# Summing attention values for twelve heads at a time instead of eight, with a third set of weight buffers, in one stage of a two-layer network

## The chip, the cores and the metric

The kernel runs on one core of a Trainium2 chip. The metric is device time in microseconds (us), the median of three runs. TensorE appears as PE in the profile (its weight loads as PEld), VectorE as DVE, ScalarE as ACT, GpSimd as POOL, SyncE, which issues most DMAs, as SP.

## The reference

Two layers on x of shape (16, 512, 128), each adding an attention-like block and an expert block to x:

```python
x = x + _L0_attn_ref(xn, ...) + _L0_ffn_ref(xn, ...)   # xn: layernorm of x
xn = _layernorm(x, axis=-1)
x = x + _L1_attn_ref(xn, ...) + _L1_ffn_ref(xn, ...)
```

The layer-0 attention is a memory that is trained by gradient steps over eight chunks. The layer-0 expert block is a convolution, a full attention of 16 heads of width 8, and eight dense experts of width 512. The change lies in the layer-1 attention, which runs a causal attention twice with the same keys and values:

```python
def _causal_attn(q, k, v):
    scores = jnp.einsum('bthd,bshd->bhts', q, k) * scale
    scores = jnp.where(mask, scores, -jnp.inf)
    attn = jax.nn.softmax(scores, axis=-1)
    return jnp.einsum('bhts,bshd->bthd', attn, v)
ctx = _causal_attn(q, k, v)
q2 = conv1d(ctx)                 # width 3, along the sequence
ctx2 = _causal_attn(q2, k, v)
out = ctx2.reshape(b, s, d) @ out_w.T + out_b
```

The layer-1 expert block routes each token to 8 of 32 experts.

## The kernel before, in words

**Turns.** The whole program is written out ahead of time by Python generators. `Turns.run` (line 284) steps every live generator once per turn, in the order of its priority; PE's order is exactly the order in which matmuls are written. Priority 0 is `tops` (`largest`, line 379): score matmuls (`s<-qx,kx`, rows 64*128) whose row maxima DVE takes (lines 396, 403, 404). Priority 1 is `back` (`weighted`, line 428): score matmuls again, transposed (`s<-kx,qx`), exponentials on ACT into a buffer `e` (line 476), the causal cut on POOL (line 484), and the value matmuls `pc<-e,vp`, which use the array as four strips of 32 columns (128*32). Later priorities hold the rest: `summed` (line 498), projections, the middle stage between the layers, and the layer-0 experts (`ffn`, line 547), whose matmuls are `phe` and `pye`. At a turn's end `fill` (line 199) adds a matmul without use if PE had little to do.

**A unit of attention.** A batch has four units in layer 1 (two passes, two halves of the heads), each of eleven turns, since a causal unit is walked in eleven steps (`widths`, line 360): four steps of width 512, four of 384, two of two times 256, one of four times 128. A step gives 2, 2, 4 or 8 heads, 32 in all. New units begin every eleven turns and a batch every 44, so the stage repeats itself every eleven turns. After the maxima of a unit, lines 410 and 411 make `mp` on DVE, PE transposes it (`tpm`, line 418), and it goes by DMA to DRAM (`top`) and back into `qx`. The unit's `back` starts some turns later and needs it.

**Values.** `weighted` keeps finished heads in the list `old`. In each step, after its scores, `tail` (line 453) looks whether at least `pools["heads"]` heads are waiting and, if so, writes value matmuls for them in groups of four, at most two groups. What is left after the eleventh step is written by `summed`. The `e` buffers come in turn from the pools in `pools["weights"]`, three from each. In layer 1 there are two pools: `att` and `mid`, later `att` and `fb`. `fb` lies where layer 0's buffers `fa` lay; it is opened when layer 0's last batch has been handed over (line 1531), but used only after the last middle stage. `lent` holds the heads whose buffer is in `mid`; the last stage begins when none is left.

**Experts.** `ffn` writes units (`first`: two matmul records of 512 columns and a ReLU on ACT; `second`: eight records of 128) as a running credit allows. Line 633 makes it write them in pairs, and none in a turn that had values, unless more than three are due.

**PSUM.** Seven banks with the tag `bank` (line 178) go round for scores and all other results; an eighth holds `pc`.

Of the kernel before, what the change touches and what calls it, by code (L numbers as in the profile page):

```python
# [73 lines left out]
def bc(ap, axis, n):  # L74

    u = ap.unsqueeze(axis)
    shape = list(u.shape)
    shape[axis] = n
    return u.to_broadcast(shape)
# [3 lines left out]
def network(ctx: ExitStack, tc: tile.TileContext, a, out):  # L83
# [56 lines left out]
    pools, done, locks, clock, newest, cleared, held, read, cell = {}, {}, set(), [0], [None], [None], [0], [0], []  # L140
# [11 lines left out]
    def acquire(name):  # L152
        while name in locks:
            yield
        locks.add(name)
# [21 lines left out]
    def work(name):  # L177
        return pools["ps"].tile([P, 512], F32, tag="bank", bufs=7, name=name)
# [10 lines left out]
    def mm(o, lhsT, rhs, start=True, stop=True):  # L189
        n = int(np.prod(rhs.shape[1:]))  # L190
        if lhsT.dtype == FR:
            load_ns[0] += 0.5 * (0.45 * n + 105)
        else:
            t = 0.42 * n if lhsT.shape[-1] == 32 and n >= P else 2 * max(0.834 * n, 110)
            load_ns[0] += t
            array_ns[0] += t
        nc.tensor.matmul(o, lhsT=lhsT, rhs=rhs, start=start, stop=stop)  # L197
# [71 lines left out]
    def ends(stage, name):  # L269
        yield from stage  # L270
        mark(*name)
# [88 lines left out]
    def widths(causal):  # L360

        for i in range(TB):
            n = S if not causal else S - i * P
            per = {S: 1, 3 * P: 1, 2 * P: 2, P: 4}[n]
            for t in range(0, NH, per):
                yield i, n, per, t
# [61 lines left out]
    def weighted(slot, vp, c, causal, cn, name):  # L428


        q, k, _ = slot
        yield from acquire("p2")
        cnv = cn.rearrange("p t (a c j d) -> p (t a) c j d", c=2, j=2, d=DH)
        old, last = [], []
        got = []

        def values(heads):
            for head in heads:
                kt, n, t, r, e = head
                lent.discard(id(head))  # L440
                g = 2 * (t % 2) + r
                j = t // 2
                mm(
                    got[0][32 * g : 32 * g + 32, S - n :], vp[:, kt, 4 * g + 2 * c + j, :], e,
                    start=(kt == 0 and j == 0), stop=(kt == TB - 1 and j == 1),
                )
            if kt == TB - 1 and t == NH - 1:
                cs = att.tile([P, S], F32, tag="cs", bufs=1, name="cs")
                nc.scalar.copy(cs, got[0])
                locks.remove("ctx")  # L450
                last.append(cs)

        def tail(least):
            if not got and "ctx" not in locks:
                locks.add("ctx")
                got.append(pools["ps"].tile([P, 512], F32, tag="ctx", bufs=1, name="pc"))
            if got and len(old) >= least:
                locks.add("values")
                for _ in range(min(len(old) // 4, 2)):
                    values([old.pop(0) for _ in range(4)])  # L460

        for i, (kt, n, per, t) in enumerate(widths(causal)):
            while len(old) >= pools["heads"] and not got and "ctx" in locks:
                yield
            s = [work("s2")[:, 0 : per * n] for r in range(2)]
            sv = [x.rearrange("p (i n) -> p i n", i=per) for x in s]
            for u in range(per):
                for r in range(2):
                    rr = slice(64 * r, 64 * r + 64)
                    mm(sv[r][:, u, :], k[rr, t + u, kt * P : (kt + 1) * P], q[rr, t + u, S - n :])  # L470
            tail(pools["heads"])

            pool = pools["weights"][i % len(pools["weights"])]
            e = pool.tile([P, 2, 512], F32, tag="e", bufs=3, name="e")
            for r in range(2):
                nc.scalar.activation(e[:, r, 0 : per * n], s[r], AF.Exp, scale=SCALE)  # L476
            ev = e[:, :, 0 : per * n].rearrange("p r (i n) -> p r i n", i=per)
            if causal:
                for r in range(2):
                    if ("counted",) in done:  # L480
                        dg = ev[:, r, :, 0:P]
                        nc.vector.scalar_tensor_tensor(dg, bc(row["tri"], 1, per), BIG, dg, ALU.mult, ALU.min)
                        continue
                    cleared[0] = nc.gpsimd.affine_select(  # L484
                        out=ev[:, r, :, 0:P], in_=ev[:, r, :, 0:P], pattern=[[0, per], [1, P]],
                        compare_op=ALU.is_ge, fill=0.0, base=0, channel_multiplier=-1,
                    )
            for u in range(per):
                for r in range(2):
                    old.append((kt, n, t + u, r, ev[:, r, u, :]))  # L490
                    if pool is pools["mid"]:
                        lent.add(id(old[-1]))
            yield
        locks.remove("p2")
        free_slots.append(slot)
        turns.stages.append((turns.turn, 2, ends(summed(old, tail, last, c, cnv), name)))

    def summed(old, tail, last, c, cnv):

        while old:  # L500
            tail(4)
            yield
        cs, = last
        yield from room()
        held[0] += 1
        tp = turn4(lambda t: cs[:, t * P : (t + 1) * P], "tpc")
        yield
        tv = tp.rearrange("p (b j x) -> p b j x", j=2, x=16)
        rec = sm.tile([P, TB * NG, 2], F32, tag="rec", name="rec")
        nc.vector.reciprocal(rec, tv[:, :, :, DH])  # L510
        nc.vector.tensor_tensor(cnv[:, :, c], tv[:, :, :, 0:DH], bc(rec, 3, DH), ALU.mult)
        drop()
        yield
# [142 lines left out]
    att = main.enter_context(tc.tile_pool(name="att", bufs=1))  # L656
# [867 lines left out]
    with tc.tile_pool(name="mid", bufs=1) as mid:  # L1524
        turns.stages += [(t0 + b * TBB, 4, middle(mid, b)) for b in range(B)]
        pools.update(weights=[att, mid], mid=mid, heads=8)
        turns.run(until=lambda: ("x1", B - 1) in done)
        turns.run(until=lambda: not any(x[1] in posts for x in turns.live))
        cell[0] = D1.t
        early.close()  # L1530
        fb = main.enter_context(tc.tile_pool(name="fb", bufs=1, side="right"))
        turns.run(until=lambda: ("xw", B - 1) in done)
        pools.update(weights=[att, fb])
        turns.run(until=lambda: not lent)
    with tc.tile_pool(name="mo", bufs=2) as mo:
        pools["work"] = 2
# [117 lines left out]
```

## Time and profile before

| what | value |
|---|---|
| median of three runs | 3565.74 us (3562.97 to 3567.28) |
| profiled execution, own time | 3557.66 us |
| its span, first to last instruction | 3555.9 us |
| DMA, mean over the span | 104 GB/s |
| score matmul records of both kinds (line 197) | 3072 + 3072 |
| value matmul records (line 197, `pc`) | 6144, busy 621.7 us |
| exponentials (line 476) | 2432, busy 1278.3 us |
| maxima, wide (line 396) and others (line 404) | 1024 and 1408 |

A matmul in float32 stands as two records, one in the kernel's fp32r form (the scores) as one. The stages, by the trace: up to about 1707 us layer 0 and the memory training, with the first layer-1 units; from there to about 3257 us layer-1 attention of the remaining batches, beside the layer-0 experts and the middle stage; then the last stage, with the routed experts, to the end.

### The profile page before, as it was taken

Reading aid. Unit: us, or ns where it says so; the run is one execution under the profiler, and the core shown is the slowest. Engines: PE = TensorE matmul, PEld = TensorE weight load, DVE = VectorE, ACT = ScalarE, POOL = GpSimd, SP = SyncE. Lnnn points to the kernel's source line nnn. Section 1 sums busy time; section 2 is a strip of 40 time slices with the busy share of each in tenths; the row PEclk is TensorE's granted clock in tenths of the full one; section 3 lists DMA queues with packets and bytes.
Section 4 is the critical chain, followed back from the end, with each engine's and each line's share of the span. In section 5 each row is a group of like instructions: output and inputs, shape, how many; then the busy total and the mean of one; then the engine's idle time right before and its main releaser. Section 6 shows DMA issues by size and latency. Waiting matters only on the chain.

```text
span 3555.9 us, 63951 instructions
## 1 busy us (share of the span) xinstructions
PE 3379.7 (95%) x22085; PEld 1897.3 (53%) x22085; DVE 2315.6 (65%) x6045; ACT 2233.4 (63%) x4951; POOL 1508.2 (42%) x2354
## 2 busy tenths in 40 slices
PE   6999999999999999999999999999999999998887
PEld 3445555554555555455555565555555555554443
DVE  5676666656766566556467667666666666567875
ACT  1566766775766787666656666665666666664444
POOL 5323432432431455432544344443444344433654
PEclk7999999999999999999999999999999999998998
DMA  5222222222122332443434443444344443433343
GB/s 178 70 71 77 71 82 74 74 77 83 56 85 86 102 109 87 133 122 102 135 108 122 124 125 115 130 126 121 107 122 122 124 125 98 134 106 98 93 102 93
DMA packets 289794, 370.37 MB, mean 104 GB/s; under 512 B 45984, under 2 KB 141376, under 8 KB 289088
## 3 DMA queue, kind: packets, MB, share of 16 engines
q1 hardware_dynamic: 282304, 359.46, 35.0%
q0 software_dynamic: 7168, 6.82, 1.2%
q8 instruction: 177, 2.90, 0.3%
q14 instruction: 145, 1.19, 0.1%
HBM read 236.58 MB, written 132.99 MB: 104 GB/s over the span
## 4 chain that ended last, share of the span: by engine, by line
PE 50%; DVE 5%; DMA 3%; ACT 1%; POOL 1%; issue 1%; SPq 1%; POOLq 0%; DVEq 0%; ACTq 0%
PE s L197 13%; PE pye L611 10%; PE phe L197 10%; PE pc L197 9%; PE pq L197 1%; DVE s L396 1%; PE fill L206 1%; DVE nm L404 1%; PE tpc L252 1%; PE tp L252 1%; DVE s L403 1%; PE po L197 1%; ACT e L476 1%; DMA rq<-lo 1%; PE pv L197 1%
## 5 line engine op out<-in xcount | busy, mean ns | idle before, releaser
L476 ACT ACTIVATE e<-s 128x512 f32<-128x512 f32 (+1 forms) x2432 | 1278.3, 577 | 556.4 <-PE s L197 517.2
L404 DVE TENSOR_REDUCE nm<-s 128x1 f32<-128x512 f32 (+2 forms) x1408 | 907.5, 682 | 510.1 <-PE s L197 509.2
L396 DVE CUSTOM_DVE_ANT_0 s<-s,sb_const 128x512 f32<-128x512 f32 (+1 forms) x1024 | 623.4, 643 | 390.3 <-PE s L197 388.9
L484 POOL TENSOR_SCALAR_AFFINE_SELECT e<-e 128x128 f32<-128x128 f32 (+2 forms) x1270 | 429.6, 347 | 751.0 <-ACT e L476 726.5
L197 PE MATMUL s<-kx,qx 64*128 64x512 f32 (+3 forms) x3072 | 620.4, 429 | 26.8 <-DMA kx<-rk 13.5
L197 PE MATMUL pc<-e,vp 128*32 128x512 f32 (+3 forms) x6144 | 621.7, 502 | 13.9 <-POOL e L484 7.8
L611 PEld LDWEIGHTS pye<-ew,hTe 128*128 128x128 f32 x4096 | 519.0, 192 | 178.7 <-issue 157.9
L197 PEld LDWEIGHTS s<-kx,qx 64*128 64x128 f32 x3072 | 271.2, 187 | 555.2 <-issue 219.4
L611 PE MATMUL pye<-ew,hTe 128*128 128x128 f32 x4096 | 562.3, 281 | 1.5 <-ACT hTe L601 1.4
L197 PE MATMUL s<-qx,kx 64*128 64x512 f32 (+3 forms) x3072 | 535.7, 356 | 27.2 <-DVE nm L404 8.4
L197 PE MATMUL phe<-x1T,ew 128*128 128x512 f32 x1024 | 551.1, 623 | 7.8 <-DMA ew<-in_ew 3.1
L601 ACT ACTIVATE hTe<-phe,sb_cols 128x512 f32<-128x512 f32 x512 | 354.1, 692 | 245.2 <-PE phe L197 242.8
L197 PEld LDWEIGHTS s<-qx,kx 64*128 64x128 f32 x3072 | 305.5, 188 | 80.4 <-ACT e L476 19.1
L619 POOL TENSOR_TENSOR ac<-ac,y 128x512 f32<-128x512 f32 x128 | 163.9, 1280 | 425.9 <-ACT y L618 363.9
L403 DVE TENSOR_TENSOR s<-s,sb_const 128x256 f32<-128x256 f32 (+1 forms) x384 | 181.6, 515 | 190.5 <-PE s L197 157.4
L197 PEld LDWEIGHTS pc<-e,vp 128*32 128x32 f32 x6144 | 151.4, 110 | 238.1 <-issue 173.2
L197 PEld LDWEIGHTS phe<-x1T,ew 128*128 128x128 f32 x1024 | 158.8, 193 | 75.0 <-issue 44.1
L618 ACT ACTIVATE y<-pye,pr 128x128 f32<-128x128 f32 x512 | 147.5, 370 | 30.6 <-PE pye L611 26.2
L396 DVE DVE_READ_ACCUMULATOR2_ANT nm<- 128x1 f32 x1024 | 144.1, 141 | 0.0
L213 POOL TENSOR_SCALAR rs_t<-ss 128x4 f32<-128x4 f32 (+1 forms) x56 | 12.0, 215 | 221.5 <-ACT sq L266 220.0
L1470 POOL DMA_INDIRECT acc<-eo,sidx x32 | 52.0, 1624 | 72.2 <-DVE eo L1464 26.3
L213 POOL TENSOR_SCALAR rs_t<-ln_mv 128x4 f32<-128x4 f32 x64 | 12.8, 200 | 162.3 <-DVE ln_mv L223 159.4
(302 smaller groups left out, 3906.4 us busy)
## 6 DMA issues: line engine op xcount, KB each, us to landing
ew<-in_ew SPq DMA_DIRECT2D x256, 256.0 KB
kx<-rk SPq DMA_DIRECT2D x192, 256.0 KB
qx<-rq SPq DMA_DIRECT2D x128, 256.0 KB
rq<-hi SPq DMA_DIRECT2D x64, 256.0 KB
rq<-lo SPq DMA_DIRECT2D x64, 256.0 KB
rk<-hi SPq DMA_DIRECT2D x64, 256.0 KB
rk<-lo SPq DMA_DIRECT2D x64, 256.0 KB
qx<-r SPq DMA_DIRECT2D x64, 256.0 KB
```

Of the source, the lines that this page charges most:

```text
L197: nc.tensor.matmul(o, lhsT=lhsT, rhs=rhs, start=start, stop=stop)
L252: nc.tensor.transpose(tp[:, t * P : (t + 1) * P], src(t), ident)
L396: newest[0] = nc.vector.tensor_tensor_reduce(out=sv[r][:, 0, :], in0=sv[r][:, 0, :], in1=row["caus"][:, S - n :], scale=1.0, scalar=-BIG, ...
L403: nc.vector.tensor_tensor(dg, dg, bc(row["caus"][:, S - P :], 1, per), ALU.add)
L404: newest[0] = nc.vector.tensor_reduce(nm[:, qt, r, t : t + per], sv[r], AX.X, ALU.max)
L476: nc.scalar.activation(e[:, r, 0 : per * n], s[r], AF.Exp, scale=SCALE)
L484: cleared[0] = nc.gpsimd.affine_select(out=ev[:, r, :, 0:P], in_=ev[:, r, :, 0:P], pattern=[[0, per], [1, P]], compare_op=ALU.is_ge, fill= ...
L601: nc.scalar.activation(hs[i], ph, AF.Relu, bias=col("fb", i))
L611: nc.tensor.matmul(pye[0][:, t, :], lhsT=h[:, t * P : (t + 1) * P], rhs=w2[e][:, f, :], start=(f == 0 and t == 0), stop=(f == 3), skip_gro ...
L618: nc.scalar.mul(y[:, t, :], pye[0][:, t, :], pr[:, t, e : e + 1])
L619: nc.gpsimd.tensor_tensor(ac, ac, y, ALU.add)
L1470: nc.gpsimd.indirect_dma_start(out=acc, out_offset=bass.IndirectOffsetOnAxis(ap=sidx[:, e : e + 1], axis=0), in_=eo[:, i, :], in_offset=No ...
```

## The change

While the middle stage still runs and layer 0's buffers are free, the `e` buffers come from three pools instead of two, and values are written when twelve heads wait, not eight; then up to three groups of four are written at once. Before that point and after the last middle stage, the numbers are those of before (four or eight heads, two groups).

```diff
@@ -456,7 +456,7 @@
             if got and len(old) >= least:
                 locks.add("values")
-                for _ in range(min(len(old) // 4, 2)):
+                for _ in range(min(len(old) // 4, max(pools["heads"] // 4, 2))):
                     values([old.pop(0) for _ in range(4)])
@@ -1529,8 +1529,9 @@
         cell[0] = D1.t
         early.close()
         fb = main.enter_context(tc.tile_pool(name="fb", bufs=1, side="right"))
+        pools.update(weights=[att, mid, fb], heads=12)
         turns.run(until=lambda: ("xw", B - 1) in done)
-        pools.update(weights=[att, fb])
+        pools.update(weights=[att, fb], heads=8)
         turns.run(until=lambda: not lent)
     with tc.tile_pool(name="mo", bufs=2) as mo:
```

## The prediction

> **What bounds the kernel now.** I read the page first, then the stage that the change touches, and then that stage turn by turn.
>
> ```profile
> span 3555.9 us, 63951 instructions
> PE 3379.7 (95%) x22085; PEld 1897.3 (53%) x22085; DVE 2315.6 (65%) x6045; ACT 2233.4 (63%) x4951; POOL 1508.2 (42%) x2354
> ```
>
> TensorE (PE) is the busy engine. The changed line takes effect after the last layer-0 batch has left (turn 574) and stops after the last middle stage (turn 1165). In the trace these turns run from 1707 to 3257 us. The busy times of that stretch alone:
>
> ```profile
> 1707.00:3257.00 1550.00, 1520.61 (x11081) 892.22 (x11079) 1015.11 (x3127) 986.38 (x2079) 692.68 (x1481) 0.99 0.42 119
> ```
>
> Columns are stretch, length, then busy time of PE, weight load, DVE, ACT and POOL, then clock, DMA share and GB/s. PE is busy 98% at a clock of 0.99, DVE 65%, ACT 64%. So the stage costs what PE's instruction stream costs, plus the short holes in it. The next view is PE and DVE in order of time, at the point where one set of maxima ends and the next begins (start, length, engine, line, operation, tiles, shapes, count):
>
> ```profile
> 642.97 1.06 PE L197 MATMUL pc<-e,vp 128*32 128x512 f32 x8
> 643.97 1.13 PE L197 MATMUL pp<-sb_pa,kT 128*128 128x256 f32 x4
> ...
> 2342.62 0.50 PE L197 MATMUL s<-kx,qx 64*128 64x512 f32 x2
> 2342.96 0.34 PE L197 MATMUL s<-qx,kx 64*128 64x384 f32 x2
> 2343.23 1.92 PE L197 MATMUL pc<-e,vp 128*32 128x512 f32 x16
> 2345.08 0.33 PE L418 MATMUL tpm<-sb_const,mp 128*128 128x128 f32 x1
> ...
> 2345.95 1.12 PE L197 MATMUL phe<-x1T,ew 128*128 128x512 f32 x2
> 2346.91 1.05 PE L611 MATMUL pye<-ew,hTe 128*128 128x128 f32 x8
> 2347.89 0.50 PE L197 MATMUL s<-kx,qx 64*128 64x512 f32 x2
> ```
>
> I go by start to next start, since ends are modelled. PE has three array shapes here: 64*128 for scores, 128*32 for values (`pc`), 128*128 for the rest; I call an unbroken run of one shape a section. One turn is scores, then values if any, then 128*128 work.
>
> **The change part by part.**
>
> *Value sections.* Eight value matmul records of four heads took 643.97 - 642.97 = 1.00 us, sixteen records of eight heads 2345.08 - 2343.23 = 1.85 us. Two small sections are thus 2 x 1.00 - 1.85 = 0.15 us dearer than one large: the price of entering and leaving the shape. A causal set of 32 heads is now summed as 8+8+8+8; with twelve it is 12+12+8. The order of the built kernel, stage alone, has 159 value sections where there were 212: 53 fewer x 0.15 = **-8.0 us**. The matmuls themselves are the same.
>
> By the Trainium skill, "TensorEngine Tiling (Array Packing)", Key Properties, a change of tiling mode drains the array; with the roughly 128-cycle drain of "TensorE: Matmul & The Clock Gate", Step-by-step, at 2.4 GHz, an estimate is two drains of 53 ns per section, -5.7 us in place of -8.0. The measured row decides.
>
> *Expert sections.* The expert planner gives a turn with values no expert work (unless over three units are due), otherwise pairs. With other turns carrying values, the order shows 14 more 128*128 sections (504 for 490): turns with a single expert unit rise from 44 to 107, turns with four fall from 18 to 1. A lone pair of 128x512 matmuls (`pjq`) took 1.06 us start to start, a lone `pye` group of eight 1.09 us, and the two shapes joined (2345.95 to 2347.89) 1.94 us: a split costs 1.06 + 1.09 - 1.94 = 0.21 us, so 14 x 0.21 = **+2.9 us**. Score sections fall by 4, under 1 us; I leave it out.
>
> *Fills.* Four more fill matmuls stand in the stage's order, on average 320 columns wide. A 512-column group inside a section costs 1.94 - 1.09 = 0.85 us, so 4 x 0.85 x 320/512 = **+2.1 us**.
>
> Work on PE: -8.0 + 2.9 + 2.1 = **-3.0 us**.
>
> *What the moved values leave uncovered.* The stage repeats every eleven turns (54 times); I number them 0 to 10 from the turn that starts a new set of maxima. Values stood in turns 0, 4, 6 and 8; now in 2, 6 and 8. Turn 0 loses its 1.85 us section. What that section covers stands on DVE:
>
> ```profile
> 2341.77 1.28 DVE L404 TENSOR_REDUCE nm<-s 128x4 f32<-128x512 f32 x2
> 2342.97 0.34 DVE L510 RECIPROCAL rec<-tpc 128x32 f32<-128x32 f32 x1
> ...
> 2344.20 0.18 DVE L411 SCALAR_TENSOR_TENSOR mp<-nm,mp 128x32 fp32r<-128x32 f32 x1
> 2344.30 0.69 DVE L396 CUSTOM_DVE_ANT_0 s<-s,sb_const 128x512 f32<-128x512 f32 x1
> 2344.91 0.14 DVE L396 DVE_READ_ACCUMULATOR2_ANT nm<- 128x1 f32 x1
> ```
>
> The narrow maxima of turn 10 end at 2343.05, 0.43 us after PE began turn 0; then `mp`, which the transpose `tpm` waits for, ends at 2344.38 and turn 0's own maxima at 2345.05. PE begins turn 1 at 2345.08: the values just cover DVE. In the changed order turn 0 has at most one expert unit in 38 of 54 cases; with one (about 1.1 us) PE would reach turn 1 at 2344.3, 0.75 us before DVE is done. Behind `tpm` in PE's queue stand the scores of turn 1, hence DVE and ACT. Seven PSUM banks absorb part. In the trace's starts and ends, PE's score matmuls stood 0.14 us longer after turns whose DVE end lay 0.6 to 0.8 us past the next turn's start (9 turns) and 0.38 us after 0.8 to 1.2 us (10 turns). Bounds: 0 if the banks take it all, 38 x 0.75 = +28 us if none. I take 0.2 us, between the two rows: 38 x 0.2 = **+8 us**.
>
> *What the moved values relieve.* Waits of the stage (engine, line, releaser, total us, times, longest):
>
> ```profile
> PEld s L197 <- ACT e L476: 60.5, 89, 0.8
> PEld pc L197 <- POOL e L484: 16.5, 43, 1.5
> PE s L197 <- DMA qx<-top: 6.5, 7, 2.0
> PE pc L197 <- POOL e L484: 3.7, 5, 1.0
> ```
>
> Line three is the maxima's way through DRAM, which starts at turn 1 and is needed at turn 7. With values moved from turn 0 into turn 2 and from 4 into 6, the work between grows by about 1.2 us, so most of the seven waits shrink: between -6.5 and 0, I take -4. Line four: the newest weights of a group are now its last of twelve heads, not of eight, some 0.7 us later, and there are fewer groups: between -3.7 and 0, I take -1. Line two is the weight load, mostly beside running matmuls; nothing. Line one: turns 3 to 5 become shorter and follow each other, turn 6 longer: between -4 and +8 on both sides by a tenth of a microsecond per period and turn; I take -1. Together **-6 us**.
>
> *Third set of buffers.* Twelve heads need up to six `e` buffers waiting; six exist, nine after. ACT's exponential then reuses a buffer nine steps old, not six, so no wait is added on ACT. The last stage's pool lies where layer 0's buffers were; its first use comes after layer 0 has ended. Nothing; at worst one wait of a few us, once. No DMA is added; SP's and POOL's orders keep their contents.
>
> *Last stage.* Its settings (eight heads, two sets) are those of before. In the built plan it begins one turn later and the whole plan has 1274 turns, not 1275. At its start PE stands idle 6.2 us for DVE, itself held until a DMA lands, so a turn more before that is hidden. Between -3 and +3; I take -1.
>
> **Sum:** -3 + 8 - 6 - 1 = **-2 us** against the profiled execution's own 3557.66 us. The runs' median is 3565.74 us; the profiled execution is 0.2% under it, so I carry the difference over: **3564 us**. About 0.2% (7 us) is what a measurement of this kernel can tell from no change.
>
> **Rivals.**
>
> *Faster: the holes close.* If the banks absorb turn 0 and the relieved waits go in full: -3 - 6.5 - 3.7 = -13, **3553 us**. For it: DVE is busy only 65% of the stage, and PE's score waits are short. Against: DVE does not rest in turns 8 to 0.
>
> *Slower: DVE takes PE's place at turn 0.* The mechanism above at 0.38 us or more in 38 periods, +14, with nothing relieved: -3 + 14 = +11, **3577 us**; at the whole 0.75 us, +25. It decides from about 0.26 us per period (7 us over 3 us of saved work, in 38 periods). For it: the DVE rows above. Against: PE's 3.9 us turn 2 lets DVE catch up, so it can't accumulate. The Trainium skill, "TensorEngine Tiling (Array Packing)", PSUM Bottleneck, warns that packed matmuls leave the reading of PSUM as the limit; the DVE rows show that for turns 8 to 0, while the stage's 65% does not.
>
> *It doesn't do what it says.* The order excludes that: 107 groups of twelve stand in it.
>
> **Chances.** Forecast 0.45, faster rival 0.27, slower rival 0.28. The range leaves out the ends of both rivals: 3550 to 3583 us. The forecast's own range, with the bounds of its small terms, is 3558 to 3572, within 0.2% either way. So faster 0.27, same 0.45, slower 0.28.
>
> **What will show it.** Right if `pc` runs of 24 records stand in turn 2 and one costs about 2.5 us, if `PE s <- DMA qx<-top` falls below 3 us, and if the waits of `s` and `tpm` for DVE grow by 5 to 10 us in the stage. If those waits grow by over 15 us the slower rival is right; if the stage falls from 1550 to under 1540 us, the faster. I am wrong if the stage before 1707 us moves, or the stage after it by more than 3 us.

## The result and the profile after

| | before | after |
|---|---|---|
| median of five runs each, same chip | 3565.74 us (3560.87 to 3567.28) | 3623.97 us (3616.69 to 3627.78) |
| profiled execution, own time | 3557.66 us | 3623.97 us |
| its span | 3555.9 us | 3622.3 us |
| PE's mean granted clock over the span | 0.975 | 0.968 |

The ratio is 1.0152 with a 95% interval of 1.0137 to 1.0166: the change makes the kernel slower, and the time lies 41 us above the predicted range's end.

The page's head, after:

```profile
span 3622.3 us, 63956 instructions
PE 3409.3 (94%) x22091; PEld 1910.5 (53%) x22091; DVE 2314.2 (64%) x6041; ACT 2226.4 (61%) x4951; POOL 1504.6 (42%) x2358
```

and the stage of the change, turns 574 to 1165, in the columns of the prediction:

```profile
1712.40:3310.90 1598.50, 1540.60 (x11096) 899.93 (x11095) 1011.88 (x3125) 981.57 (x2079) 689.18 (x1481) 0.98 0.41 115
```

and before, between the same turns:

```profile
1706.70:3256.90 1550.20, 1520.81 (x11082) 892.42 (x11081) 1015.01 (x3125) 986.65 (x2079) 692.88 (x1481) 0.99 0.42 119
```

What the reader is to see: the stage is 48.3 us longer (1550.2 before), while DVE's busy time is 3 us less than before and ACT's 5 us. No engine has more to do, apart from the 20 us that PE's busy time grew. Length less busy time of PE went from 29.4 to 57.9 us: 28.5 us more in which PE stood idle. The clock explains most of the rest. Summed over the stretches of the stage in which the records show PE at half clock, before had 34.1 us in six and after has 64.9 us in ten; half of a stretch is lost, so this is 15 of the 20 us.

The other 18 us of the two spans' difference of 66.4 us lie outside the stage: 5.7 us before it, 5.8 us between it and PE's last record, and 6.6 us behind that record. Up to the stage PE's order is the same in both kernels and in the experiments e1 to e4 and e8 to e10, yet the stage's first transpose (`tp<-sb_const,x`) starts anywhere from 1706.5 to 1719.9 us in these runs (before 1707.3, after 1713.0). e1, whose whole PE order is that of before, takes 6.9 us longer than before from its last transpose `tp<-sb_const,xwt`, near the stage's end, to the end. So the part ahead of the stage is no larger than what executions of one order differ by, and the part behind it not clearly larger. The medians differ by 58.2 us.

**Which turns.** Mean length in us of the turns of the stage's 54 periods, numbered as in the prediction, from the starts of PE's records:

| turn | 0 | 1 | 2 | 3 | 4 | 5 | 6 | 7 | 8 | 9 | 10 | sum |
|---|---|---|---|---|---|---|---|---|---|---|---|---|
| before | 2.97 | 2.45 | 2.82 | 2.21 | 2.23 | 2.80 | 2.10 | 3.38 | 2.37 | 2.60 | 2.82 | 28.75 |
| after | 2.92 | 2.79 | 4.18 | 1.98 | 2.27 | 2.24 | 2.71 | 2.60 | 2.49 | 2.70 | 2.74 | 29.62 |

The sum grows by 0.87 us, 54 times: 47 us. Turn 0 is the odd one. It lost a value section of 1.85 us, gained about one expert unit of 1.1 us, and is still nearly as long as it was. To separate work from waiting I took, for each pair of neighbouring PE records, the spacing that the same pair of forms has in before when neither is held, and called what lies above it the hole (it holds the idle time, and matmuls that run at a lower clock). Turn 0's hole went from 0.23 to 1.04 us, turn 1's from 0.15 to 0.35, turn 6's from 0.29 to 0.41, turn 7's fell from 0.37 to 0.23, and the others stayed within 0.05 us. Turns 0 and 1 together: (0.81 + 0.20) x 54 = **55 us**.

**What stands there.** In the rows, `s<-kx,qx` are the scores whose maxima DVE takes and `s<-qx,kx` the transposed ones for the exponentials (in turn 0 they are 512 and 384 wide); the description of the kernel above has these two names the other way round. PE in order of time at one turn 0 without values (start, length, engine, line, operation, tiles, count, and in brackets the idle time before and what ended it):

```profile
2757.52 0.45 PE L197 MATMUL s<-qx,kx 64*128 64x512 f32 x2
2757.90 1.16 PE L611 MATMUL pye<-ew,hTe 128*128 128x128 f32 x8
2758.89 1.02 PE L197 MATMUL phe<-x1T,ew 128*128 128x512 f32 x2
2759.85 0.50 PE L197 MATMUL s<-kx,qx 64*128 64x512 f32 x2
2760.18 0.65 PE L197 MATMUL s<-qx,kx 64*128 64x384 f32 x2
2761.65 0.63 PE L252 MATMUL tp<-sb_const,cn 128*128 128x128 f32 x4 [0.82 <-DVE mp L411]
2762.12 1.06 PE L611 MATMUL pye<-ew,hTe 128*128 128x128 f32 x8
2763.01 0.27 PE L418 MATMUL tpm<-sb_const,mp 128*128 128x128 f32 x1
```

and DVE at the same time:

```profile
2759.00 1.28 DVE L404 TENSOR_REDUCE nm<-s 128x4 f32<-128x512 f32 x2
2760.19 0.35 DVE L510 RECIPROCAL rec<-tpc 128x32 f32<-128x32 f32 x1
2760.45 0.12 DVE L410 TENSOR_SCALAR mp<-nm 128x32 fp32r<-128x32 f32 x1
2760.48 0.69 DVE L396 CUSTOM_DVE_ANT_0 s<-s,sb_const 128x512 f32<-128x512 f32 x1
...
2761.09 0.42 DVE L511 TENSOR_TENSOR cn<-tpc,rec 128x256 f32<-128x256 f32 x1
2761.42 0.18 DVE L411 SCALAR_TENSOR_TENSOR mp<-nm,mp 128x32 fp32r<-128x32 f32 x1
```

DVE is still at the narrow maxima of turn 10 until 2760.28. Behind them in its queue stand `rec` and `cn`, the scaling of the finished context, and `mp`. PE has done the scores of turn 0 by 2760.83 and next in its queue is `tp`, the transpose of `cn`. `cn` ends at 2761.51 and `mp` at 2761.60; `tp` starts at 2761.65. The expert unit `pye`, which the prediction took for cover, stands behind `tp` in PE's queue and waits with it (in most periods without `tp`, an expert unit stands ahead of `tpm`, and the hole is smaller). In before, eight heads' values stood between the scores and `tp`, and DVE was done when they were; a turn 0 of before with a `tp`:

```profile
2312.66 0.34 PE L197 MATMUL s<-qx,kx 64*128 64x384 f32 x2
2312.93 1.92 PE L197 MATMUL pc<-e,vp 128*32 128x512 f32 x16
2314.78 0.66 PE L252 MATMUL tp<-sb_const,cn 128*128 128x128 f32 x4
2315.27 0.27 PE L418 MATMUL tpm<-sb_const,mp 128*128 128x128 f32 x1
```

The waits of the stage, after (engine, line, releaser, total us, times, longest):

```profile
PEld s L197 <- ACT e L476: 76.6, 105, 2.2
PEld pc L197 <- POOL e L484: 35.4, 97, 1.9
PE tp L252 <- DVE cn L511: 11.7, 12, 2.1
PE tpm L418 <- DVE mp L411: 9.2, 14, 1.9
PE tp L252 <- DVE mp L411: 8.0, 7, 1.9
...
PE pc L197 <- POOL e L484: 5.4, 11, 1.4
PE s L197 <- DMA qx<-top: 4.5, 3, 2.5
```

The three lines of `tp` and `tpm` sum to 28.9 us. The same three in before:

```profile
PE tpm L418 <- DVE mp L411: 1.0, 3, 0.4
PE tp L252 <- DVE mp L411: 0.6, 1, 0.6
...
PE tp L252 <- DVE cn L511: 0.3, 1, 0.3
```

They are 1.9 us in all. The difference, 27 us, is nearly the whole growth of PE's idle time. The other 28 of the 55 us are matmuls that stood longer without a wait of a matmul that the trace names.

### The profile page after: what moved, and what is told of

The parts are those of the page before. It is cut to its first block, busy times and chain, and to the rows that moved or that the text cites. A ratio compares the mean times of both kernels' runs of the same rounds, so it can differ in the third digit from the quotient of the medians.

```text
span 3622.3 us, 63956 instructions
## 1 busy us (share of the span) xinstructions
PE 3409.3 (94%) x22091; PEld 1910.5 (53%) x22091; DVE 2314.2 (64%) x6041; ACT 2226.4 (61%) x4951; POOL 1504.6 (42%) x2358
## 5 line engine op out<-in xcount | busy, mean ns | idle before, releaser
L396 DVE CUSTOM_DVE_ANT_0 s<-s,sb_const 128x512 f32<-128x512 f32 (+1 forms) x1024 | 624.6, 643 | 477.8 <-PE s L197 476.7
L611 PE MATMUL pye<-ew,hTe 128*128 128x128 f32 x4096 | 570.5, 283 | 1.0 <-ACT e L476 0.6
L396 DVE DVE_READ_ACCUMULATOR2_ANT nm<- 128x1 f32 x1024 | 145.5, 142 | 0.0
```

The costliest lines, as they stand in the source:

```text
L396: newest[0] = nc.vector.tensor_tensor_reduce(out=sv[r][:, 0, :], in0=sv[r][:, 0, :], in1=row["caus"][:, S - n :], scale=1.0, scalar=-BIG, ...
L611: nc.tensor.matmul(pye[0][:, t, :], lhsT=h[:, t * P : (t + 1) * P], rhs=w2[e][:, f, :], start=(f == 0 and t == 0), stop=(f == 3), skip_gro ...
```

## The experiments

Theory A: the value section of turn 0 was the cover for DVE's lateness, and without it `tp` and `tpm` wait. Rivals: B, groups of twelve heads are themselves dear (their weights come late, or a long section starves ACT and DVE); C, the third set of buffers costs time. Each ratio is against runs of before on the same chip, with its 95% interval.

**e1, the third set alone.** Groups stay at eight heads, the number in force just ahead of the stage. Edit to before:

```diff
+        pools.update(weights=[att, mid, fb])
         turns.run(until=lambda: ("xw", B - 1) in done)
-        pools.update(weights=[att, fb])
+        pools.update(weights=[att, fb], heads=8)
```

> The kernel before with the third set of weight buffers alone: groups of eight as before. The order of its TensorE instructions is that of the kernel before. Theory A (the value section that stood in turn 0 covered VectorE; without it TensorE waits there): 3566 us, within 7 us of before. Theory B (groups of twelve are too long: ACT and VectorE run dry, and weights come too late from GpSimd): 3566 us as well. Theory C (the third set itself, its place and the changed rotation, costs the time): about 3615 us.

Measured: 3570.80 us against 3570.92, ratio 0.9995 (0.9982 to 1.0007). C falls.

**e2, the old group sizes, turn 0 uncovered.** Edit to before: the group that is due in turn 0 is written one turn later (`late` is set in the changed stage alone; `i` is the step, and step 4 stands in turn 0).

```diff
-            tail(pools["heads"])
+            if not (i == 4 and pools.get("late")):
+                tail(pools["heads"])
```

> The kernel before, two sets, groups of eight, four value sections for each unit; only the first group, in the changed stage, is written in turn 1 in place of turn 0. Its order has 49 fewer 128*128 sections (1004 for 1053), some 10 us less work at 0.21 us each. Theory A: turn 0 loses its cover as in the changed kernel, 0.8 us in 54 periods, +43, and turn 1 gets the 1.85 us section as cover: between 3590 and 3610 us. Theory B: no group is longer, so 3555 to 3570 us. Theory C: 3555 to 3570 us.

Measured: 3602.40 us, ratio 1.0093 (1.0071 to 1.0115). Nothing in it is longer than eight heads, and it has two sets of buffers, yet turn 0's hole is 0.92 us and the same waits appear:

```profile
PE tp L252 <- DVE mp L411: 12.0, 9, 2.4
...
PE tp L252 <- DVE cn L512: 9.0, 10, 2.1
PE tpm L418 <- DVE mp L411: 6.8, 10, 2.1
```

A is needed for this and B cannot give it.

**e3, long groups with turn 0 covered.** Groups of 8, 16 and 8 heads, the first in turn 0, with three sets. Edit to before; the second number given to `tail` is the most groups of four that it writes at once:

```diff
+            if pools.get("late") and i >= 8:
+                tail(16, 4)
+            else:
+                tail(pools["heads"])
```

> Three sets and three value sections for each unit as in the change, but the first of eight heads in turn 0, then sixteen heads in one section in turn 6, then eight. 53 fewer value sections (-8 us), 44 more 128*128 sections (+9 us). Theory A: turn 0 keeps its cover: 3560 to 3575 us. Theory B: a group of sixteen is longer still: 3620 us or more. Theory C: about 3615 us.

Measured: 3561.47 us, ratio 0.9978 (0.9966 to 0.9991), turn 0's hole 0.31 us. Groups longer than twelve cost no more than they save, so B falls as the cause; as many value sections are saved as in the change, and here the sum is a small gain.

**e4, the same with groups of 8, 12 and 12.** `tail(16, 3)` from step 8 on, and `summed` writes the last twelve:

```diff
-            tail(4)
+            tail(4, 3)
```

> Three sets, groups of eight (in turn 0), twelve (turn 6) and twelve (at the end of the unit). 53 fewer value sections, 41 more 128*128 sections. Theory A: 3560 to 3575 us. Theory B: two groups of twelve for each unit as in the change: about 3620 us. Theory C: about 3615 us.

Measured: 3557.16 us, ratio 0.9960 (0.9948 to 0.9972), 3 us under the range of theory A. The stage, between the same turns as above, and its waits:

```profile
1715.40:3248.70 1533.30, 1508.36 (x11080) 890.30 (x11079) 1015.84 (x3125) 981.39 (x2079) 689.83 (x1481) 0.99 0.43 120
```

```profile
PE s L197 <- DMA qx<-top: 7.5, 4, 3.8
...
PE tpm L418 <- DVE mp L411: 1.5, 4, 0.6
```

The stage is 65 us shorter than with the change and 17 us shorter than before, PE's idle time is 24.9 us, the waits of `tp` and `tpm` for DVE are about 2 us, and the half-clock stretches fall to 20 us in three. This version is faster than both kernels.

**e5 and e6, DVE less late.** The sum of scores and mask ahead of the narrow maxima (turns 8 to 10) goes, in before (e5) and in the change (e6):

```diff
-                if causal:
-                    dg = sv[r][:, :, n - P : n]
-                    nc.vector.tensor_tensor(dg, dg, bc(row["caus"][:, S - P :], 1, per), ALU.add)
```

> The kernel before without the causal cut ahead of the narrow maxima (widths 256 and 128, VectorE additions of line 403): the row maxima then also see scores that the causal cut later drops; the softmax doesn't depend on which bound is subtracted. It takes about 1.3 us of VectorE from each of turns 8, 9 and 10 and nothing from TensorE. It is the base for the next run. Theory A: TensorE is the bound and VectorE was covered: 3550 to 3570 us. Theory B says the same.

> The changed kernel without the same VectorE additions. Theory A (TensorE waits in turn 0 because VectorE is still at the maxima of turns 8 to 10): VectorE is done 1 to 3 us earlier, and the loss against the run before it (the kernel before without these additions) falls from 58 to under 20 us. Theory B (the long groups themselves): the loss stays at 50 to 60 us.

Measured: e5 3548.24 us, ratio 0.9935 (0.9910 to 0.9960); e6 3562.83 us, ratio 0.9990 (0.9976 to 1.0004). With DVE relieved the same change costs 14.6 us, not 58, turn 0's hole is 0.28 us, and the waits of `tp` and `tpm` for DVE are 5.1 us. The loss hangs on DVE's lateness, as A says. e5 itself came out 2 us under the range that both theories gave: DVE's lateness cost something in before too, where turn 0 was covered.

**e7, the 8, 12, 12 groups without that sum.** e4's edit and e5's:

```diff
+            if pools.get("late") and i >= 8:
+                tail(16, 3)
...
-                    nc.vector.tensor_tensor(dg, dg, bc(row["caus"][:, S - P :], 1, per), ALU.add)
```

> Groups of eight, twelve and twelve, and the additions left out as well: the two together. Theory A: VectorE's lateness is covered already, so little is added: 3545 to 3560 us. If VectorE's lateness costs elsewhere too (turns 8 to 10): under 3545 us.

Measured: 3533.74 us, ratio 0.9896 (0.9869 to 0.9922), 14.5 us less than e5, about what e4 gains on before. What these groups save is there with the sum and without it, as long as turn 0 is covered. The time lies under 3545 us, the mark set down for a lateness that costs elsewhere too: leaving the sum out gains about 0.65%, in before (e5) as with these groups. Where it costs was not followed.

**e8, the transposes of a context a turn later.** In the two generators that take a unit pair's result on, one idle turn ahead of its transposes where groups are of twelve. Edit to the change, in both places:

```diff
+        if pools["heads"] == 12:
+            yield from idle(1)
```

> The changed kernel with one edit: in the changed stage the transpose of a unit pair's result (tp from cn, in half of the turns 0) is written one turn later. Theory A, first form (that transpose is the first to wait for VectorE and stands ahead of the expert matmuls that could have covered it): about 0.9 us less in 25 periods, 3598 to 3608 us. Second form (whoever stands first in TensorE's queue waits, next the transpose tpm): 3615 to 3630 us.

Measured: 3656.40 us, ratio 1.0245 (1.0219 to 1.0271), outside what either theory gave. `tp` no longer waits for `cn` or `mp`, and `tpm` waits 18.4 us for `mp` in the stage where it waited 9.2, but the idle turns delayed what comes after them too: over the whole run the projection `pjq` waits 41.1 us for its input by DMA in 14 places, with the change 2.0 us, once, in the stage. Too much moved at once; the run decides nothing.

**e9, DVE's queue reordered, PE's order kept.** In `summed`, `rec` and `cn` are written as soon as their source is there, so ahead of the last maxima:

```diff
-        yield
+        early = pools["heads"] == 12
+        if not early:
+            yield
...
+        if early:
+            yield
```

> The changed kernel with TensorE's order exactly as it was, matmul for matmul; only VectorE reads the sums of a unit (reciprocal and product, rec and cn) ahead of the maxima of turn 10 instead of behind them, in the changed stage. Theory A, first form (in turn 0 the transpose of cn is what waits, and nothing takes its place): its wait for cn and mp, 24 us in the changed kernel, goes, and some of the half-clock time with it: 3590 to 3603 us. Second form (the next in the queue, tpm, waits for the maxima that now end later): 3610 to 3630 us. Theory B (long groups): no change, 3624 us.

Measured: 3593.02 us, ratio 1.0092 (1.0069 to 1.0115), hole of turn 0 about 0.7 us. The waits:

```profile
PE tpm L418 <- DVE mp L411: 22.7, 23, 2.9
PE pc L197 <- POOL e L484: 5.4, 11, 1.4
```

`tp` no longer waits for `cn` or `mp`, and `tpm`, the next in PE's queue that does, has taken over part: 22.7 us instead of 9.2. Of the loss, 21 us by the ratios and 27 us by the medians come back. The time lies in the range of A's first form, while the wait went where the second form put it. So one part of the loss is the place of `cn` behind the maxima in DVE's queue, and another is that `mp` must stand behind them, since it is made of them.

**e10, PE's time in turn 0 filled.** One matmul without use, 512 columns wide, after the scores of turn 0:

```diff
+            if i == 4 and pools["heads"] == 12 and held[0] < pools["work"]:
+                o = work("fill")
+                nc.tensor.matmul(o, lhsT=ident, rhs=cell[0][:, 0:512], start=True, stop=True)
```

> The changed kernel with one matmul without use, 512 columns, 1.06 us, behind the scores of turn 0 in each period of the changed stage (53 of them, 56 us of TensorE work). Theory A (TensorE stands idle there anyway and the holes cost clock besides): the work falls into the holes, 3600 to 3635 us, with fewer half-clock stretches. Theory B (TensorE is not waiting in turn 0; the cost lies in the long groups): 56 us more, 3670 to 3685 us.

Measured: 3612.23 us, ratio 1.0150 (1.0128 to 1.0173). The stage:

```profile
1706.70:3301.80 1595.10, 1562.33 (x11202) 907.07 (x11201) 1013.74 (x3125) 979.46 (x2079) 689.22 (x1481) 1.00 0.40 116
```

53 fills of 1.06 us, 56 us of matmul, cost nothing that can be told from the change's own 1.0152. They took the place of two things: PE's idle time in the stage fell from 57.9 to 32.8 us, with 4 us of waits of `tp` and `tpm` for DVE in place of 28.9, and the half-clock stretches fell from 64.9 to 13.7 us, half of which, 26 us, had been lost. PE had the time of the fills to spare.

**e11, e7 with e9's reading.** The edits of both, with `late` in place of twelve heads as the mark of the stage:

> Groups of eight, twelve and twelve, no cut ahead of the narrow maxima, and the sums of a unit read early as in the run above. Turn 0 is covered already, so theory A gives little: 3522 to 3538 us.

Measured: 3528.94 us, ratio 0.9911 (0.9888 to 0.9935), no different from e7. Where the cover is kept, the earlier reading is worth nothing.

**e12, the change with both of DVE's reliefs.** e6's and e9's edits:

> The changed kernel with both reliefs of VectorE at once: no causal cut ahead of the narrow maxima, and the sums of a unit read early. TensorE's order is still that of the changed kernel. It shows what of the loss is left when turn 0 has nothing to wait for; its base is the kernel before without the cut (0.9935 of before). If all the loss is VectorE's lateness: 0.992 to 0.996 of before. If some 15 us belong to the long groups of twelve (weights late from GpSimd in turn 6, VectorE and ACT idle in turn 2): 0.997 to 1.001.

Measured: 3549.83 us, ratio 0.9963 (0.9949 to 0.9977), hole of turn 0 0.20 us. That is between the two forecasts. The change's loss against e5 (0.9935, on another chip) shrinks to about 0.3%; the two intervals allow 0 to 0.6%. Two waits of the stage:

```profile
PE pc L197 <- POOL e L481: 5.6, 11, 1.4
PE tpm L415 <- DVE mp L408: 2.8, 2, 1.7
```

`tpm`'s wait is nearly gone, and the values' wait for weights that POOL cuts is about 2 us above before's 3.7. That is a small part of what is left; the rest of it, some 8 us if it is there at all, stays open.

## Why the prediction was wrong, step by step

- **What the moved values leave uncovered, +8 us: this is the step that failed.** The mechanism was the right one and stood as the slower rival ("DVE takes PE's place at turn 0"), but its size was off. The term was 0.2 us in 38 periods; the trace shows 1.0 us in 54, +55 us in turns 0 and 1, beyond even the upper bound of +28. Three things went into that:
  - *The wrong waiter.* The price was read from score matmuls, whose own waits for DVE stayed small with the change too (`PE s <- DVE nm L396`: 1.7 us, 4 times, in the stage). First in PE's queue after turn 0's scores stand `tp` (in 25 of the 54 periods) and `tpm`, whose operand is DVE's result itself, so that a free bank doesn't help them. Turn 0's mean hole is 1.46 us where it has `tp`, 0.73 us where not. The prediction named `tpm` as a waiter, and then priced by others.
  - *The wrong cover.* Expert units were counted as cover in every turn 0 that has one. They are written ahead of `tpm`, where they do cover, but behind `tp`, as the rows at 2761.65 and 2762.12 show. In the periods with `tp` they cover nothing of its wait.
  - *The clock.* Holes were taken at their own length. The waits of `tp` and `tpm` alone, 28.9 us, lie just at the upper bound; what goes beyond it are matmuls that stood longer without such a wait. The half-clock stretches of the stage cost 32 us after and 17 before, 15 us that no term held (those that fall in turns 0 and 1 are in the 55 us, so they are not to be added).
- **The argument against that rival, a turn 2 of 3.9 us that lets DVE catch up.** Turn 2 did become long (4.18 us), but it comes after turn 0. DVE is late because of turns 8 to 10 before it, and nothing in the new order lies between these and `tp`.
- **PE's work, -3 us.** The sections fell as counted (in the traces 212 to 159 for values, 490 to 504 for 128*128). What they are worth was not measured alone. In e3 and e4 the 53 fewer value sections stand beside 44 and 41 more 128*128 sections, so by the prediction's prices the sum would be about nothing; measured are gains of 0.2% and 0.4%. Something is saved there, but which price is off stays open: 7 of the 17 us by which e4's stage is shorter than before's are fewer half-clock stretches. In the change any saving is buried.
- **What the moved values relieve, -6 us.** Of it, 2 us came: `s <- DMA qx<-top` went from 6.5 to 4.5 us, against the 2.5 or less that was named. The values' wait for POOL rose from 3.7 to 5.4 us, and that of their weight loads from 16.5 to 35.4, where a fall and nothing were named. A twelve-head group does wait for fresher weights; this is the part of B that is true, at about 2 us of matmul waits.
- **The third set, nothing.** Right, by e1.
- **The last stage, -1 us.** The part behind the stage is 12.4 us longer, in one profile of each kernel; 6.9 us of difference there come without any change of PE's order (e1), so whether the rest is the change's stays open.
- **What will show it.** The signs shared the wrong waiter. By their words, the waits of `s` and `tpm` for DVE, the growth is 7 us (4.1 to 11.2, matmuls alone), in the band set down for the forecast being right; only with `tp`, which they don't name, is it over the 15 us of the slower rival: 26 us. A section of 24 records, now in turn 2, costs 2.50 us, as named (2766.37 to 2768.87). The condition that the stage's start must not move was no good test, since it lies up to 13 us apart in executions of the same order of work.

More than half of it could have been read from before. In the rows that the prediction shows, the scores of turn 0 end at 2343.23 and `mp`, behind `cn`, at 2344.38:

```profile
2343.87 0.42 DVE L511 TENSOR_TENSOR cn<-tpc,rec 128x256 f32<-128x256 f32 x1
```

With the section gone and `tp` next in the queue, that is 1.15 us of hole, in 25 periods 29 us; measured in these periods are (1.46 - 0.27) x 25 = 30 us. In the other 29 periods one expert unit of 1.1 us should leave next to nothing by the same rows; measured are (0.73 - 0.16) x 29 = 17 us, of which the waits of `tpm` are 8 to 9, and 11 us in turn 1. (For turn 0 the means over all periods give 44 us in place of 30 + 17; the split is that rough.) How much of these 28 us is the clock and how much DVE's lateness handed on was not separated.

## What to carry to other kernels

Before a stretch of work is moved on a busy engine, look which other engine is late where the stretch stood, and what is first in the queue behind it: if that instruction needs the late engine's own result, the whole lateness becomes a hole, whatever lies further back. Price such a hole by that waiter's operand, row against row, not by mean waits or busy shares (DVE is busy 63% of this stage and still sets the end of turn 0). Groups of 8, 12 and 12 heads, which leave the cover in place, gained 0.4%.

## What the runs showed of the hardware

Holes cost more than their length, because the granted clock falls to half behind some of them, in stretches of 3.4 us or small multiples (6.8, 10.2, 13.7). Each of the 16 stretches in the stages of before and after begins inside a hole of 0.9 to 3.1 us or less than 2 us behind one; other holes of that size have none behind them. The same four matmuls in before, behind a hole that a DMA made (granted clock 0.50 from 2463.0 to 2473.2 us), and elsewhere (1.00):

```profile
2463.80 3.75 PE L197 MATMUL phe<-x1T,ew 128*128 128x512 f32 x4 [3.11 <-DMA ew<-in_ew]
```

```profile
2309.61 1.98 PE L197 MATMUL phe<-x1T,ew 128*128 128x512 f32 x4
```

Matmuls without use in the hole keep the clock up: e10 has 13.7 us of half clock in the stage where the change has 64.9, and its mean clock there is 1.00. But this returned no time that can be told, since the fills' own time stands against it. At 0.85 us each inside a section (the prediction's figure) to 1.06 us alone, an estimate is 45 to 56 us, and the idle time and the half clock that they took away are 25 and 26 us. In e4, where a section of values that are needed stands in that place, half clock fell to 20 us and the time came back.
